# Another order for the first five tiles of a gated cross-attention and expert kernel

## The chip, the cores and the metric

The kernel runs on one core of a Trainium2 chip. Its time is the device time of one execution in microseconds (us); the median of three runs stands for the kernel. One further execution was recorded by the hardware profiler, and all times of single instructions come from it. The engines are PE (matmuls, with PEld for the loading of weights), DVE (vector), ACT (activations), POOL (general, and the issuer of indirect DMAs) and SP (issuer of plain DMAs).

## The reference

There are 4 sequences of 512 tokens, each token a vector of 256. Cut to what matters:

```python
def attend(q, kv_src, seg_id, Wq, Wkv, Wo):          # 16 heads of 16
    qh = split_heads(q @ Wq.T)
    k, v = split(kv_src @ Wkv.T, 2)
    gather = seg_id[:, :, None] - arange(4)          # four rows of kv_src for each token
    scores = einsum(qh, k[gather]) * 16 ** -0.5      # masked where gather < 0
    return einsum(softmax(scores), v[gather]) @ Wo.T

def experts(x, gate_w, w1, b1, w2, b2):              # 8 experts, 256 -> 1024 -> 256
    probs = softmax(x @ gate_w.T)
    weight = probs where among the two largest, else 0
    return sum_e weight[e] * (silu(x @ w1[e] + b1[e]) @ w2[e] + b2[e])

x = x + tanh(g_xattn) * attend(layernorm(x), ctx, itok, Wq, Wkv, Wo)
x = x + tanh(g_ffn) * experts(layernorm(x), ...)
```

All numbers are float32.

## The kernel before

The 2048 tokens are 16 tiles of 128. The kernel has two parts that overlap. The first goes over the tiles: attention, then the gate, then a scatter of every token's normalised row into a table `xs` in DRAM, once into the region of each of its two experts. The second goes over 37 blocks of 128 rows: it reads a block of `xs`, computes one expert on it, and adds the result to the output with an indirect DMA. A block can be read when the gate has been computed for enough tiles that it is surely full; the first three blocks are sure after tile 4 (`RAMP = 5`), and two more after each tile.

For a tile `t` the stages are these.

- `rows_of(t)`: an indirect DMA on POOL gathers the four rows of keys and values of each token into `g` (three buffers, 1 MB each; issued two tiles ahead). It reads a table `near` of the sequence, which `project_near` makes: a product on PE, a copy on ACT (`kv_near`), two stores by SP.
- `stage_ask(t)`: PE computes `pq`, the query and a part of the gate; ACT copies the gate's part to `asked`.
- `stage_attend(t)`: DVE computes `prod`, `sc` and the shifted scores; ACT the exponential `ex` (L459); DVE the sum `sm`, the weights `pr` and `v`. For the first four tiles the four parts of `v` are added on PE, later on DVE (`ao`). The generator yields twice before the sum, so that other work can be put in.
- `stage_out(t)`: PE transposes to `pa` (L497, L499), ACT copies to `aoT` (L512), PE computes `po` (L515), and DVE adds it to `x_sb` (L518), makes the gate's logits and the moments.
- `stage_route(g)`: for a group `g` of one or two tiles (tiles 0 and 1, tiles 2 and 3, then 4, 5, 6 and 7 alone): SP stores `x_sb`; DVE takes the two best experts (`best`, `which`, `pick`); PE counts ranks in `pp` (L568, L571); POOL computes the inverse root `rs` (`v_b` L266, `rs` L268) and writes the token numbers (L586); ACT the exponentials `exg` and the rows (L609); DVE the positions (`place`, `pos`), `nm` and the weights; and POOL issues two scatters for each tile (L377).
- `queue(tiles, w)`: DVE computes which expert and which row of `xs` the next `w` blocks take (`expert`, `row`). SP reads these, and fetches the block's weights `w1s` and its rows `xg`.

In a block PE transposes (`pxg` L783), DVE copies (`xgT` L786), PE computes the first product `ph` (L798), ACT the silu (L810), PE the second product `py` (L825).

The order on an engine is decided by a scheduler at build time, except that `in_order` chains the instructions traced within it: those of DVE only, when it is called without engines. `behind` puts one instruction behind another. The PSUM pool `ps_m` has two buffers, shared by `pa`, `po`, `pp` and the products of the near tables. SP also loads `xT`, `x` and the second weights `w2_sb`, where the loads of step `i` are tied to `prod` of tile `i` (`seen[i]`).

Of the kernel before, what the change touches and what calls it, by code (L numbers as in the profile page):

```python
# [23 lines left out]
def gated_xattn_moe(  # L24
# [29 lines left out]
    NT = NTOK // P  # L54
# [6 lines left out]
    RAMP = 5  # L61
    GROUPS = [(sum(sizes[:i]), n) for i, n in enumerate(sizes)]
    EDGE = KW - 1
    LKW = LKV + 2 * EDGE
    TOPK = 2
# [4 lines left out]
    PE, SP = mybir.EngineType.PE, mybir.EngineType.SP  # L70
# [3 lines left out]
    @contextmanager  # L74
    def in_order(*engines):

        traced = nc.cur_bb.bb.instructions
        old = {i.name for i in traced}
        yield
        for i in nc.cur_bb.bb.instructions:  # L80
            if i.name not in old and i.engine in (engines or (mybir.EngineType.DVE,)):
                if i.engine in order:
                    tc.add_manual_dep(i, order[i.engine].name, ORDER, reason="in this order")
                order[i.engine] = i
# [45 lines left out]
    src_rest = early_tile(KD * (B - 1) * P, "p (k b c) -> p k b c", k=KD, b=B - 1)  # L130

    def behind(i, *others, dep=ORDER):
        for other in others:
            tc.add_manual_dep(i, other.name, dep, reason="not in the way")
# [95 lines left out]
    def project_near(kv, psum, src, b, after=None):  # L230
        project(kv, psum, src, P, near[b], EDGE, f"near{b}", after)
        queue = nc.scalar if b == 0 else nc.sync
        return queue.dma_start(
            out=near[b][0:EDGE, :].unsqueeze(0),
            in_=kv[0:1, :].unsqueeze(1).to_broadcast([1, EDGE, 2 * D]),
        ).ins
# [48 lines left out]
    with tc.tile_pool(  # L285
# [26 lines left out]
        for m in range(KD):  # L312
            for k in range(KD):
                i = nc.tensor.matmul(
                    pwg[:, m, :],
                    wo_o[:, k, ts(m, P)],
                    wqg_sb[:, k, D:DG],
                    start=(k == 0),
                    stop=(k == KD - 1),
                ).ins  # L320
# [31 lines left out]
    def _layers(ctx, is_near):  # L352
# [10 lines left out]
        ps_m = pool("ps_m", 2, True)  # L363
# [7 lines left out]

        scatters, reads = [], []

        def scatter(rows, where):
            i = nc.gpsimd.indirect_dma_start(  # L377
                out=xs,
                out_offset=bass.IndirectOffsetOnAxis(ap=where, axis=0),
                in_=rows,  # L380
                in_offset=None,
            ).ins
            for other in scatters + reads:
                tc.declare_no_dep(i, other, reason="rows of their own")
            scatters.append(i)
# [24 lines left out]
        gathered, ops, asked, seen, exps, mvs, logits = {}, {}, {}, {}, {}, {}, {}  # L410
        group_of = {t: (g, t - t0) for g, (t0, n) in enumerate(GROUPS) for t in range(t0, t0 + n)}

        def rows_of(t):
            gt = gat.tile([P, KW, 2 * D], F32, tag="g", name=f"g_{t}")
            if is_near:
                i = gather_near(gt, t)
            else:
                i = gather(gt, every, B * LKW, idx_every[:, t : t + 1])
            gathered[t] = gt
            return i  # L420

        def stage_ask(t):

            pq = ps_q.tile([P, DG], F32, tag="q", name=f"pq_{t}")
            for k in range(KD):
                nc.tensor.matmul(  # L426
                    pq, xT_sb[:, t, k, :], wqg_sb[:, k, :], start=(k == 0), stop=(k == KD - 1)
                )
            asked[t] = small.tile([P, E], F32, tag="asked", name=f"asked_{t}")
            nc.scalar.copy(asked[t], pq[:, D:DG])  # L430
            ops[t] = pq
# [57 lines left out]
        def stage_out(t):  # L489
            ao = ops.pop(t)  # L490
            pa = ps_m.tile([P, KD, P], F32, tag="m", name=f"pa_{t}")
            parts = ao.shape[1]
            traced = len(nc.cur_bb.bb.instructions)
            for k in range(KD):
                for o in range(parts):
                    if parts == 1:
                        nc.tensor.transpose(pa[:, k, :], ao[:, o, ts(k, P)], ident)  # L497
                    else:
                        nc.tensor.matmul(  # L499
                            pa[:, k, :],  # L500
                            ao[:, o, ts(k, P)],
                            ident,
                            start=(o == 0),
                            stop=(o == parts - 1),
                        )
            if RAMP <= t and t + 1 in seen:

                for i in nc.cur_bb.bb.instructions[traced:]:
                    if i.engine == PE:
                        behind(i, seen[t + 1])  # L510
            aoT = att.tile([P, KD, P], F32, tag="aoT", name=f"aoT_{t}")
            nc.scalar.copy(aoT, pa)  # L512
            po = ps_m.tile([P, DG], F32, tag="m", name=f"po_{t}")
            for k in range(KD):
                nc.tensor.matmul(  # L515
                    po, aoT[:, k, :], wo_sb[:, k, :], start=(k == 0), stop=(k == KD - 1)
                )
            nc.vector.scalar_tensor_tensor(  # L518
                x_sb[:, t, :], po[:, 0:D], tg[:, 0:1], x_sb[:, t, :], ALU.mult, ALU.add
            )  # L520
            g, j = group_of[t]
            if j == 0:
                mvs[g] = stat.tile([P, GMAX, 2], F32, tag="mv", name=f"mv_{g}")
                logits[g] = gate.tile([P, GMAX, E], F32, tag="lg", name=f"lg_{g}")

            nc.vector.tensor_tensor(logits[g][:, j, :], po[:, D:DG], asked.pop(t), ALU.add)
            moments(mvs[g][:, j, :], x_sb[:, t, :], f"b{t}")


        def stage_route(g):  # L530

            t0, GT = GROUPS[g]
# [8 lines left out]
            row = gate.tile([P, GMAX, ROW], F32, tag="rows", name=f"rows_{g}", bufs=3)[:, 0:GT]  # L541
# [21 lines left out]
            for j in range(GT):  # L563
                t = t0 + j
# [14 lines left out]
            rs = stat.tile([P, GMAX], F32, tag="rs", name=f"rs_{g}")[:, 0:GT]  # L579
            nm = stat.tile([P, GMAX], F32, tag="nm", name=f"nm_{g}")[:, 0:GT]  # L580
            root = rsqrt(rs, mv, GT, f"b{g}")
            if t0 == RAMP - 1:

                for i in scatters[-TOPK * GROUPS[g - 1][1] // 2 :]:
                    behind(i, root)
            named = nc.gpsimd.tensor_copy(  # L586
                row_meta[:, :, :, 1].bitcast(I32),
                tokid[:, tiles].unsqueeze(2).to_broadcast([P, GT, E]),
            ).ins
            behind(named, root)  # L590
            for j in range(GT):
                nc.scalar.activation(ex[:, j, :], ex[:, j, :], AF.Exp, scale=rs[:, j : j + 1])
            yield
# [10 lines left out]
            pos = gate.tile([P, GMAX, TOPK], I32, tag="pos", name=f"pos_{g}")[:, 0:GT]  # L604
# [26 lines left out]
                tc.declare_no_dep(weighted, i, reason="other columns")  # L631
            for j in range(GT):
                for c in range(TOPK):
                    scatter(row[:, j, :], pos[:, j, c : c + 1])
            yield


# [247 lines left out]
        AHEAD = 2  # L885
# [10 lines left out]
        before = 0  # L896
        for i in range(NT + 1):
            if i + AHEAD < NT:
                gathers.append(rows_of(i + AHEAD))
            attend = stage_attend(i) if i < NT else iter(())  # L900
            queued = surely(i) if i in ends else 0
            with in_order():

                next(attend, None)
                if i != RAMP:
                    next(attend, None)
                if i < RAMP:
                    for _ in attend:
                        pass
                if i:  # L910
                    stage_out(i - 1)
                if i + 1 < NT:
                    stage_ask(i + 1)
                if i in ends:
                    for _ in stage_route(ends[i]):
                        pass
                if i >= RAMP and queued:
                    queue(i, queued - before)
                    before = queued
                if i == NT:  # L920
                    queue(i, NS - before, last=True)
                if i in (0, RAMP, RAMP + 2):
                    normalise_first(1 + (i + 1) // TPB)
                for _ in attend:
                    pass
            if is_near and i == 0:
                for b in range(1, B):
                    project_near(
                        kv_near[:, b, :], ps_m, src_rest[:, :, b - 1, :], b, after=exps[0]
                    )  # L930
            if i < E // 2:

                loads = [load_xT(i + 1), load_x(i + 2)] if i + 2 < B else []
                if i + 2 == B:
                    loads.append(load_xT(i + 1))
                for e in (2 * i, 2 * i + 1):
                    loads.append(nc.sync.dma_start(out=w2_sb[:, ts(e, NF), :], in_=w2[ts(e, P), :]).ins)
                for load in loads:
                    behind(load, seen[i], dep=SYNC)
# [91 lines left out]
```

## Time and profile before

| what | value |
|---|---|
| median of 3 runs | 398.99 us (397.7 to 399.93) |
| profiled execution: its own time | 399.22 us |
| profiled execution: span from first to last instruction | 397.5 us |
| mean granted clock of PE in it | 0.942 |
| busy: PE, DVE, ACT, POOL | 343.4, 195.7, 160.1, 131.3 us |
| first product of block 0 (`ph`) starts at | 85.24 us |

A line of the timeline reads: start in us, duration in us, engine, line of the code, operation, output and inputs with their shapes, count, and in brackets the idle time of the engine before it and what ended it. In the row of slices each digit is the busy share of a fortieth of the span (9.94 us) in tenths; `PEclk` is the granted clock of PE in tenths.

### The profile page before, as it was taken

Reading aid. Unit: us, or ns where it says so; the run is one execution under the profiler, and the core shown is the slowest. Engines: PE = TensorE matmul, PEld = TensorE weight load, DVE = VectorE, ACT = ScalarE, POOL = GpSimd, SP = SyncE. Lnnn points to the kernel's source line nnn. Section 1 sums busy time; section 2 is a strip of 40 time slices with the busy share of each in tenths; the row PEclk is TensorE's granted clock in tenths of the full one; section 3 lists DMA queues with packets and bytes.
Section 4 is the critical chain, followed back from the end, with each engine's and each line's share of the span. In section 5 each row is a group of like instructions: output and inputs, shape, how many; then the busy total and the mean of one; then the engine's idle time right before and its main releaser. Section 6 shows DMA issues by size and latency. Waiting matters only on the chain. (4 is left out here: it accounts for less than half of the span.)

```text
span 397.5 us, 7304 instructions
## 1 busy us (share of the span) xinstructions
PE 343.4 (86%) x2153; PEld 306.9 (77%) x2153; DVE 195.7 (49%) x663; ACT 160.1 (40%) x445; POOL 131.3 (33%) x164
## 2 busy tenths in 40 slices
PE   4877646089999989999999999999999999999960
PEld 1545534078998989898889989999999999999950
DVE  2288797879789989798947301101111111111000
ACT  1121202027756666767576334234243342342410
POOL 4421444513365354453724322112112122121311
PEclk9869696579999999999999999999999999999995
DMA  7899999589969988987667897776767767755111
GB/s 259 269 399 423 419 425 378 177 287 313 299 187 343 237 274 280 336 238 233 205 158 189 281 222 234 236 196 164 246 176 211 214 171 235 195 167 143 18 28 17
DMA packets 43577, 94.22 MB, mean 237 GB/s; under 512 B 14844, under 2 KB 31996, under 8 KB 35720
## 3 DMA queue, kind: packets, MB, share of 16 engines
q1 hardware_dynamic: 33506, 66.23, 51.2%
q0 software_dynamic: 9168, 26.09, 23.0%
q10 hardware_dynamic: 854, 1.33, 1.0%
q8 instruction: 21, 0.34, 0.3%
q14 instruction: 28, 0.23, 0.2%
HBM read 79.90 MB, written 13.73 MB: 236 GB/s over the span
## 5 line engine op out<-in xcount | busy, mean ns | idle before, releaser
L798 PE MATMUL ph<-xgT,w1s 128*128 128x128 f32 x1184 | 143.0, 276 | 0.0
L798 PEld LDWEIGHTS ph<-xgT,w1s 128*128 128x128 f32 x1184 | 140.3, 192 | 2.3
L825 PE MATMUL py<-w_sb,hT 128*128 x592 | 135.7, 380 | 1.4 <-DVE yw L836 0.7
L810 ACT ACTIVATE hT<-ph,b1s 128x128 f32<-128x128 f32 x296 | 83.6, 372 | 113.6 <-issue 95.7
L825 PEld LDWEIGHTS py<-w_sb,hT 128*128 128x128 f32 x592 | 109.2, 190 | 15.7 <-issue 2.1
L839 POOL DMA_INDIRECT out<-yw,ms x37 | 58.7, 1586 | 158.3 <-issue 69.5
L836 DVE SCALAR_TENSOR_TENSOR yw<-py,ms,b2s 128x256 f32<-128x256 f32 x37 | 17.8, 482 | 76.3 <-PE py L825 72.4
L786 DVE COPY xgT<-pxg 128x256 f32<-128x256 f32 x37 | 15.6, 421 | 69.5 <-PE pxg L783 69.4
L377 POOL DMA_INDIRECT xs<-rows,pos x32 | 35.0, 1094 | 30.6 <-ACT rows L609 7.3
L240 POOL DMA_INDIRECT g<-near,idx_near x16 | 17.6, 1098 | 37.4 <-DVE v L472 23.3
L439 DVE TENSOR_TENSOR prod<-pq,g 128x1024 f32<-128x1024 f32 x16 | 19.4, 1213 | 5.9 <-DMA g<-near,idx_near 5.9
L426 PE MATMUL pq<-wqg_sb,xT_sb 128*128 128x264 f32 x64 | 20.5, 449 | 1.5 <-DVE prod L439 1.1
L515 PE MATMUL po<-wo_sb,aoT 128*128 128x264 f32 x64 | 19.8, 436 | 2.0 <-ACT aoT L512 1.4
L472 DVE TENSOR_TENSOR v<-g,pr 128x1024 f32<-128x1024 f32 x16 | 19.6, 1224 | 0.5
L810 ACT ACT_TABLE_LOAD x13 | 16.7, 1283 | 7.7 <-issue 5.2
L442 DVE TENSOR_REDUCE sc<-prod 128x64 f32<-128x1024 f32 x16 | 19.5, 1217 | 0.4
L868 ACT ACTIVATE b2s<-b2s,ms 128x256 f32<-128x256 f32 x37 | 19.5, 532 | 0.0
L426 PEld LDWEIGHTS pq<-wqg_sb,xT_sb 128*128 128x128 f32 x64 | 14.0, 225 | 5.2 <-DVE prod L439 2.2
L497 PE MATMUL pa<-ident,ao 128*128 128x128 f32 x24 | 5.6, 308 | 13.2 <-DVE ao L485 13.1
L515 PEld LDWEIGHTS po<-wo_sb,aoT 128*128 128x128 f32 x64 | 12.1, 207 | 5.6 <-ACT aoT L512 4.0
L783 PE MATMUL pxg<-ident,xg 128*128 128x128 f32 x74 | 14.5, 278 | 1.5 <-DMA xg<-xs 1.5
L497 PEld LDWEIGHTS pa<-ident,ao 128*128 128x128 f32 x24 | 3.3, 165 | 14.5 <-issue 11.6
(128 smaller groups left out, 262.6 us busy)
## 6 DMA issues: line engine op xcount, KB each, us to landing
w1s<-in_w SPq DMA_DIRECT2D x37, 1024.0 KB, 5.4
w_sb<-in_w SPq DMA_DIRECT2D x8, 1024.0 KB
b2s<-in_b SPq DMA_DIRECT2D x37, 128.0 KB, 5.2
xg<-xs SPq DMA_DIRECT2D x37, 128.0 KB, 5.5
xT_sb<-in_xT SPq DMA_DIRECT2D x4, 512.0 KB, 11.3
x_sb<-in_x SPq DMA_DIRECT2D x4, 512.0 KB
out<-x_sb SPq DMA_DIRECT2D x6, 256.0 KB
xs<-padrow SPq DMA_DIRECT2D x9, 136.0 KB, 3.7
```

The costliest lines, as they stand in the source:

```text
L377: i = nc.gpsimd.indirect_dma_start(out=xs, out_offset=bass.IndirectOffsetOnAxis(ap=where, axis=0), in_=rows, in_offset=None,).ins
L426: nc.tensor.matmul(pq, xT_sb[:, t, k, :], wqg_sb[:, k, :], start=(k == 0), stop=(k == KD - 1))
L439: seen[t] = nc.vector.tensor_tensor(prod, pq[:, 0:D].unsqueeze(1).to_broadcast([P, KW, D]), gt[:, :, 0:D], ALU.mult).ins
L442: nc.vector.tensor_reduce(sc.rearrange("p o h -> p (o h)"), prod.rearrange("p o (h d) -> p (o h) d", d=HD), AX.X, ALU.add,)
L472: nc.vector.tensor_tensor(v.rearrange("p o (h d) -> p o h d", d=HD), gt[:, :, D : 2 * D].rearrange("p o (h d) -> p o h d", d=HD), pr.unsqu ...
L515: nc.tensor.matmul(po, aoT[:, k, :], wo_sb[:, k, :], start=(k == 0), stop=(k == KD - 1))
L798: m = nc.tensor.matmul(ph[:, i, :], w1s[:, k, ts(f, P)], xgT[:, k, :], start=(k == 0), stop=(k == KD - 1),).ins
L810: hidden = nc.scalar.activation(hT[:, f, :], ph[:, i, :], AF.Silu, bias=b1s[:, f : f + 1]).ins
L825: m = nc.tensor.matmul(py, hT[:, f, :], w2_sb[:, bass.ds(be_v * NF + f, 1), :].rearrange("p o d -> p (o d)"), start=(f == 0), stop=(f == N ...
L836: outs[s] = nc.vector.scalar_tensor_tensor(yw, py, ms[:, 0:1], b2s, ALU.mult, ALU.add).ins
L839: acc = nc.gpsimd.indirect_dma_start(out=out, out_offset=bass.IndirectOffsetOnAxis(ap=ms[:, 1:2].bitcast(I32), axis=0), in_=yw, in_offset= ...
L868: behind(nc.scalar.activation(b2s, b2s, AF.Copy, scale=ms[:, 0:1]).ins, hidden)
```

## The change

It touches the order of work in the first five tiles, and a little behind them.

- `stage_out` is cut into three: the transposes and the copy, `stage_project` (the product `po`) and `stage_add` (the sum, the logits and the moments).
- In tiles 0 to 4 the transposes of tile `i` come in step `i` itself, ahead of the ranks of the group that ends there, and its `po` behind these ranks. The sum of tile `i - 1` comes in step `i` behind the shifted scores, where ACT computes the exponential.
- In step 5 the products `prod` and `sc` of tile 5 are no longer taken first: the sum and the route of tile 4, the queue and the moments of the third sequence come ahead of them.
- The tables `near` of sequences 1 to 3 are made one each in steps 0, 1 and 2, instead of all three in step 0.
- PE's order is chained in steps 0 to 4, and POOL's in steps 0 to 5, gathers with it.
- The two scatters of tile 3 are held, and traced behind the `rs` and the token numbers of tile 4; before, `behind` put them behind that `rs`.

```diff
-        scatters, reads = [], []
+        scatters, reads, held = [], [], []
...
             nc.scalar.copy(aoT, pa)
+            ops[t] = aoT
+
+        def stage_project(t):
+            aoT = ops.pop(t)
             po = ps_m.tile([P, DG], F32, tag="m", name=f"po_{t}")
             for k in range(KD):
                 nc.tensor.matmul(
                     po, aoT[:, k, :], wo_sb[:, k, :], start=(k == 0), stop=(k == KD - 1)
                 )
+            ops[t] = po
+
+        def stage_add(t):
+            po = ops.pop(t)
             nc.vector.scalar_tensor_tensor(
...
-            if t0 == RAMP - 1:
-
-                for i in scatters[-TOPK * GROUPS[g - 1][1] // 2 :]:
-                    behind(i, root)
...
             behind(named, root)
+            while held:
+                scatter(*held.pop())
...
-                    scatter(row[:, j, :], pos[:, j, c : c + 1])
+                    if t0 + GT == RAMP - 1 and j:
+
+                        held.append((row[:, j, :], pos[:, j, c : c + 1]))
+                    else:
+                        scatter(row[:, j, :], pos[:, j, c : c + 1])
...
             if i + AHEAD < NT:
-                gathers.append(rows_of(i + AHEAD))
+                with in_order(*([mybir.EngineType.Pool] if i <= RAMP else [])):
+                    gathers.append(rows_of(i + AHEAD))
...
-            with in_order():
-
-                next(attend, None)
+            engines = [mybir.EngineType.DVE]
+            engines += [PE] if i < RAMP else []
+            engines += [mybir.EngineType.Pool] if i <= RAMP else []
+            with in_order(*engines):
+
                 if i != RAMP:
                     next(attend, None)
+                    next(attend, None)
+                if i > RAMP:
+                    stage_out(i - 1)
+                    stage_project(i - 1)
+                if i:
+                    stage_add(i - 1)
+                if i + 1 < NT:
+                    stage_ask(i + 1)
                 if i < RAMP:
                     for _ in attend:
                         pass
-                if i:
-                    stage_out(i - 1)
-                if i + 1 < NT:
-                    stage_ask(i + 1)
-                if i in ends:
-                    for _ in stage_route(ends[i]):
-                        pass
+                    stage_out(i)
+                route = stage_route(ends[i]) if i in ends else iter(())
+                next(route, None)
+                if i < RAMP:
+                    stage_project(i)
+                for _ in route:
+                    pass
+                if is_near and i + 1 < B:
+                    project_near(
+                        kv_near[:, i + 1, :], ps_m, src_rest[:, :, i, :], i + 1, after=exps[i]
+                    )
...
-            if is_near and i == 0:
-                for b in range(1, B):
-                    project_near(
-                        kv_near[:, b, :], ps_m, src_rest[:, :, b - 1, :], b, after=exps[0]
-                    )
```

## The prediction

> **What bounds the kernel now.** I read the page's slices first. PE is full from slice 8 (85 us) to the end and mostly idle before: the blocks of experts are a matmul stream, and what comes ahead of it only decides when it starts and with what beside it.
>
> ```profile
> PE   4877646089999989999999999999999999999960
> PEclk9869696579999999999999999999999999999995
> ```
>
> So I took the timeline of each engine from 20 us to the first block. PE shows how the stream starts: after 11 idle us come the transposes of block 0, then tile 5's output and tile 7's query, all at half clock (32 matmuls of `ph` take 3.73 us later, and four of `po` 1.16), then the first products at 85.24.
>
> ```profile
> 79.80 0.66 PE L497 MATMUL pa<-ident,ao 128*128 128x128 f32 x2 [10.67 <-DVE ao L485]
> 81.41 0.69 PE L783 MATMUL pxg<-ident,xg 128*128 128x128 f32 x2 [0.95 <-DMA xg<-xs]
> 81.89 1.97 PE L515 MATMUL po<-wo_sb,aoT 128*128 128x264 f32 x4
> 83.65 1.75 PE L426 MATMUL pq<-wqg_sb,xT_sb 128*128 128x264 f32 x4
> ```
>
> PE waited for xg, which SP could issue only at 79.32, when the last scatters had landed; the weights were asked for at 72.40.
>
> ```profile
> 72.40 0.37 SPq L752 DMA_DIRECT2D w1s<-in_w  x1
> 79.32 0.33 SPq L770 DMA_DIRECT2D xg<-xs  x1
> ```
>
> The scatters come from POOL, whose timeline shows no slack here: six scatters, one rsqrt and a copy in a row, with gaps of 0.2 to 0.3.
>
> ```profile
> 64.88 1.10 POOL L377 DMA_INDIRECT xs<-rows,pos  x1 [3.28 <-ACT rows L609]
> 66.29 0.97 POOL L377 DMA_INDIRECT xs<-rows,pos  x1 [0.30 <-issue]
> 67.53 0.19 POOL L266 TENSOR_SCALAR v_b<-mv 128x1 f32<-128x1 f32 x1 [0.27 <-DVE best L547]
> 67.80 0.62 POOL L268 TENSOR_TENSOR rs<-v_b,mhalf 128x1 f32<-128x1 f32 x1
> 68.61 1.06 POOL L377 DMA_INDIRECT xs<-rows,pos  x1 [0.20 <-issue]
> ...
> 72.71 0.96 POOL L377 DMA_INDIRECT xs<-rows,pos  x1 [0.30 <-issue]
> ```
>
> Ahead of that DVE is the bound, busy but for the exponential and the ranks (`sm`, `place`). Its lines for tile 4, and the copy and exponential of ACT beside them:
>
> ```profile
> 53.62 0.37 ACT L512 COPY aoT<-pa 128x256 f32<-128x256 f32 x1 [1.54 <-PE pa L499]
> 55.64 0.35 ACT L459 ACTIVATE ex<-sc,rsa 128x64 f32<-128x64 f32 x1 [1.65 <-DVE sc L455]
> 56.02 0.26 DVE L462 TENSOR_REDUCE sm<-ex 128x16 f32<-128x64 f32 x1 [0.41 <-ACT ex L459]
> 66.28 0.47 DVE L518 SCALAR_TENSOR_TENSOR x_sb<-po,tg,x_sb 128x256 f32<-128x256 f32 x1
> 69.44 0.15 DVE L607 SCALAR_TENSOR_TENSOR nm<-mv,rs 128x1 f32<-128x1 f32 x1
> ```
>
> **The change part by part.** No compute is added or taken away; all is order. I read the new order from the built program, engine by engine, and lay before's durations on it. The figure followed is the start of the six scatters, 64.88.
>
> *Outputs added while exponentials run, tiles 1 to 4.* The waits for the exponential (0.56, 0.41, 0.42, 0.41) go. But tile t-1's output is now added 3.27 us after its v ends (prod 1.22, sc 1.22, three small ones), and it is ready only after the transposes 2.02, copy 0.37, output 1.16 and four hand-overs, 3.9 at full clock. Tile 1: pa starts cold at 25.95 and output is there near 31.6, against 31.15: wait 0.5 for 0.56, 0. Tile 2: wait 0.6 for 0.41, +0.2. Tile 3: the route lies between, no wait, -0.4. Tile 4: ACT's new order has tile 4's exponential ahead of tile 3's aoT, which in before was copied at 53.62, two us earlier than it. So aoT starts 0.3 after `sc` is done, and output follows: 0.66 + 0.06 + 1.16 + 0.05 = 1.93 wait for 0.41: +1.5, and +2.5 if PE has gone cold (PE would be idle 3.4 us before it). I take +1.9.
>
> *Transposes ahead of ranks.* Ranks of tiles 0 and 1 now stand behind 2.02 us of pa, while picks take 1.7: wait 1.1 for 1.26, as PE is warm. Ranks of tiles 2 and 3 stand behind two transposes: 0.57 for 0.90. Together -0.5.
>
> *The near tables*, projected one per tile. On SP their stores stand behind the loads tied to tiles 0 and 1. Up to the first store 5.5 MB stand in SP's queue from 21.3 and 3.1 MB in POOL's; at the 0.42 MB/us of the saturated stretch (DMA share near 1.0 from 20 to 67) it lands near 42, where before it was there at 31. Tile 4's gather is held until then on POOL (issued at 34.38 before), and the rsqrt of tiles 0 and 1 behind it (41.80 before): rs near 45, when DVE's nm wants it: +0.4, between 0 and +2. The gather then has until 52 (9.2 us is its median): covered, with nothing to spare if it is issued after 43. The third near store waits for ACT at 48, with tile 12's xT and four w2 loads behind it (41.33 before): w2 is first read after 90, hidden; the DMA backlog that ended at 67.5 may end some 2 us later, under the first scatters.
>
> Start of the scatters: 0 + 0.2 - 0.4 + 1.9 - 0.5 + 0.4 = +1.6, 66.5.
>
> *Tile 4's output ahead of tile 5's products.* The 2.45 us of prod and sc leave DVE's way, and PE's output lies under the route: add at about 65.4 instead of 66.28. That gain meets POOL. Its new order from the first scatter on is scatter, scatter, the gather of tile 7 (issued at 58.36 before, 1.29 long), v_b, scatter, rs, copy, three scatters. The gather adds 1.5 with its gap, the third scatter 1.3 ahead of rs. So rs ends 3.54 + 2.8 = 6.35 after the start: 72.85. DVE's nm waits for it (69.44 before) and all of the queue (row, w1s' number) behind it: +3.4, w1s at 75.8, landing (5.4) by 81.2. Of the scatters the last ends 8.79 + 1.5 = 10.3 after the start, 76.8 for 73.67. From there to xg's issue 5.65 as before (w1s stands in the same place to them): 82.4. The early output is spent waiting.
>
> *The start of the stream.* xg lands 2.1 later, pxg 84.5, copied (0.42) by 85.65: first products at 85.7, for 85.24. But before had by then also done pa, po and pq; now they stand inside block 0, because tile 5 comes later: 0.4 + 1.05 + 1.05 = 2.5 at full clock. And in before they used up the cold clock; now block 0's products do. Clock rows: work from 42.91 was at full clock near 47.5, from 24.26 near 30.4, from 63.51 near 68, from 81.41 near 85.0: 3.6 to 6.2, mean 4.7, half lost: 2.35. The Trainium skill ("TensorE: Matmul & The Clock Gate", Part 1) says one busy window of about 3.4 us releases the clock, a loss of 1.7 at half rate; it also says that the window runs free of the program, so the wait may be longer. The trace's starts were longer, so I take 2.35; by 3.4 us the sum is 0.65 less.
>
> *After that* tile 5 is later by about what the stream is. DVE gets two copies of xgT put ahead of ranks and queue and waits for PE there; xg of block 3 (issued 99.07, used 104.60) has about its landing time of 5.5. I take +0.5 for stalls, 0 to +3. ACT gets 8 more table loads of 1.28 (59 for 51 over both branches of the program): covered by its idle time, half the stream. Regrouped later tiles: 0, within 1.
>
> Sum: 0.45 + 2.5 + 2.35 + 0.5 = +5.8. The profiled execution took 399.22 (span 397.5), 0.23 over the median; taken from 398.99 that is 404.8. A measurement of this kernel tells about 0.5%, 2.0 us, from no change.
>
> **Rivals.** *Faster: POOL's order doesn't bind.* If the spans of POOL's DMA instructions are mostly drawn and not spent, rs of tile 4 comes before 67.6, and the earlier output passes through. It decides there. Then DVE sets the chain; with the four exponential waits gone as meant (-1.8) and the 2.45 out of the way, products could start at 82.6 - 4.3 = 78.3; with pa, po, pq and the cold clock (4.9) that is 83.2 for 85.24: -2.0, 397.0. For it: POOL's spans are rough. Against it: before's third scatter started exactly where rs let it, and each next start is one span and 0.3 on.
>
> *No change.* The scatters start 0.9 early in the warm case of tile 4 and without the near wait, and land in 3.5 (median 4.7, least 2.4) instead of 5.65, if w1s comes behind them: 3.05 less than my sum, 0.65 less from the clock and no stalls (0.5): +1.6, 400.6. Against it: w1s and last scatter hang on the same rs.
>
> *Slower still: the near tables.* Gather 4 issued at 45 holds rs of tiles 0 and 1 until 47 (+2), and tile 4's products wait for its landing (+1), and blocks 3 and 5 stall: 405 + 3 = 408. For it: SP's queue is full to 67; against it: I count 42, not 45.
>
> **How the numbers follow.** Main case 0.62 (402 to 407), slower still 0.17, no change 0.14, faster 0.07. Predicted 404.8. The range takes in the main case and most of the slow one and the no-change one: 399.5 to 409.0; left out are the faster case and the ends, under 0.2. Slower by over 0.5% 0.79, within 0.14, faster 0.07.
>
> **What would show it.** POOL: six scatters from about 66.5 with a gather after the second, and rs of tile 4 ending near 73. DVE: a wait of 3 to 5 us at nm of tile 4 for POOL, and about 1.9 at tile 3's add for PE. PE: block 0's products about 85.7 at half clock, with pa, po and pq among them. ACT: aoT of tile 3 right behind an exponential. Wrong: nm without a wait, or the first products before 83; then the gather's place on POOL cost nothing. If the loss is there but nm is on time, it is in the near tables or the stream's stalls.

## Result and the profile after

The changed kernel takes 421.15 us (median of 4 runs, 420.47 to 421.38), the kernel before on the same chip 398.71. The ratio is 1.0559, with a 95% interval of 1.0526 to 1.0592: slower by 22.4 us, where +5.8 was predicted, and outside the stated range of 399.5 to 409.0. The profiled execution took 421.38 (span 419.7; before 399.22).

The slices of the page (10.5 us each, counted from 0) show that the stream of blocks still begins in slice 8, and that it now has gaps, in slice 10 (from 105 us) and slice 16 (from 168), with the clock low in slices 11 and 17, behind them.

```profile
PE   5448574289699989499999999999999999999970
PEclk9759965569969999979999999999999999999996
```

POOL's timeline has the order that was read from the built program: the gather after two scatters, `rs` of tile 4 behind a third.

```profile
67.41 1.10 POOL L377 DMA_INDIRECT xs<-rows,pos  x1 [5.53 <-ACT rows L615]
68.81 0.98 POOL L377 DMA_INDIRECT xs<-rows,pos  x1 [0.30 <-issue]
70.10 0.99 POOL L240 DMA_INDIRECT g<-near,idx_near  x1 [0.30 <-issue]
71.16 0.19 POOL L266 TENSOR_SCALAR v_b<-mv 128x1 f32<-128x1 f32 x1
71.62 1.01 POOL L377 DMA_INDIRECT xs<-rows,pos  x1 [0.27 <-issue]
72.65 0.60 POOL L268 TENSOR_TENSOR rs<-v_b,mhalf 128x1 f32<-128x1 f32 x1
...
76.38 0.96 POOL L377 DMA_INDIRECT xs<-rows,pos  x1 [0.30 <-issue]
```

DVE's timeline has the two waits that the prediction named, for PE at the add of tile 3 and for POOL at `nm` of tile 4. The second is shorter than the 3 to 5 us that were named, since DVE itself comes there later: the output of tile 4 is added at 67.22, not at 65.4.

```profile
58.72 0.48 DVE L526 SCALAR_TENSOR_TENSOR x_sb<-po,tg,x_sb 128x256 f32<-128x256 f32 x1 [2.92 <-PE po L519]
73.28 0.16 DVE L613 SCALAR_TENSOR_TENSOR nm<-mv,rs 128x1 f32<-128x1 f32 x1 [2.41 <-POOL rs L268]
```

PE's timeline shows the first products at half clock (ten take 2.50, and 1.28 before), with tile 5's output among them.

```profile
85.03 0.69 PE L793 MATMUL pxg<-ident,xg 128*128 128x128 f32 x2 [2.44 <-DMA xg<-xs]
86.24 2.50 PE L808 MATMUL ph<-xgT,w1s 128*128 128x128 f32 x10 [0.52 <-DVE xgT L796]
90.24 1.76 PE L519 MATMUL po<-wo_sb,aoT 128*128 128x264 f32 x4
```

So far it is the forecast. What it lacked is in PE's waits from 75 us on (columns: total, times, longest). Before, the same line read 1.5 us in two times.

```profile
PE pxg L793 <- DMA xg<-xs: 14.5, 5, 5.9
```

Blocks are counted from 0. In the kernel before PE had no wait at block 3:

```profile
104.60 0.38 PE L783 MATMUL pxg<-ident,xg 128*128 128x128 f32 x2
104.82 3.62 PE L825 MATMUL py<-w_sb,hT 128*128 x16
```

The two large waits of the changed kernel, at blocks 3 and 9, with what follows them on PE:

```profile
114.61 0.41 PE L793 MATMUL pxg<-ident,xg 128*128 128x128 f32 x2 [4.05 <-DMA xg<-xs]
114.86 2.94 PE L835 MATMUL py<-w_sb,hT 128*128 x8
...
119.72 5.00 PE L808 MATMUL ph<-xgT,w1s 128*128 128x128 f32 x32
...
179.37 0.66 PE L793 MATMUL pxg<-ident,xg 128*128 128x128 f32 x2 [5.93 <-DMA xg<-xs]
179.94 5.62 PE L835 MATMUL py<-w_sb,hT 128*128 x16
```

At full clock 8 `py` take 1.89, 16 take 3.62 and 32 `ph` 3.73. Block 3's wait costs 4.05 and about 3.3 of slow products, block 9's 5.93 and 2.0. Start of the transposes of a block (us), in the two kernels and in two of the experiments below:

| block | before | after | e1: tile 5 first again | e2: before, tile 5 last |
|---|---|---|---|---|
| 0 | 81.41 | 85.03 | 83.90 | 80.48 |
| 3 | 104.60 | 114.61 | 107.87 | 110.97 |
| 4 | 111.84 | 124.56 | 115.12 | 119.01 |
| 8 | 152.18 | 163.03 | 155.48 | 158.43 |
| 10 | 170.31 | 191.66 | 173.63 | 186.90 |

Why block 3's rows are late: ACT's timeline beside blocks 0 and 1. Between a silu and an exponential there stands a table load (`ACT_TABLE_LOAD`) each time.

```profile
89.99 1.28 ACT L820 ACT_TABLE_LOAD   x1
91.29 1.15 ACT L820 ACTIVATE hT<-ph,b1s 128x128 f32<-128x128 f32 x4
92.45 1.28 ACT L459 ACT_TABLE_LOAD   x1
93.75 0.35 ACT L459 ACTIVATE ex<-sc,rsa 128x64 f32<-128x64 f32 x1
94.10 1.28 ACT L820 ACT_TABLE_LOAD   x1
95.39 1.14 ACT L820 ACTIVATE hT<-ph,b1s 128x128 f32<-128x128 f32 x4
96.56 1.28 ACT L598 ACT_TABLE_LOAD   x1
97.85 0.30 ACT L598 ACTIVATE exg<-exg,rs 128x8 f32<-128x8 f32 x1
98.17 1.28 ACT L820 ACT_TABLE_LOAD   x1
...
102.18 0.63 ACT L615 ACTIVATE rows<-x_sb,nm,rs 128x256 f32<-128x256 f32 x1
```

In the kernel before, ACT did the exponential of tile 6, the gate's exponential and the rows of tile 5 ahead of the first silu:

```profile
84.53 0.35 ACT L459 ACTIVATE ex<-sc,rsa 128x64 f32<-128x64 f32 x1 [3.61 <-DVE sc L455]
...
86.57 0.30 ACT L592 ACTIVATE exg<-exg,rs 128x8 f32<-128x8 f32 x1 [0.97 <-POOL rs L268]
87.75 0.60 ACT L609 ACTIVATE rows<-x_sb,nm,rs 128x256 f32<-128x256 f32 x1 [0.88 <-DVE nm L607]
88.37 1.28 ACT L810 ACT_TABLE_LOAD   x1
89.67 2.18 ACT L810 ACTIVATE hT<-ph,b1s 128x128 f32<-128x128 f32 x8
```

POOL's timeline of the changed kernel has `rs` of tile 5 early, and then POOL stands idle for 9.28 us until those rows are there. (The bracket names DVE's `took`, which ended last, but in both kernels this scatter starts 0.79 after the rows end.)

```profile
93.58 0.59 POOL L268 TENSOR_TENSOR rs<-v_b,mhalf 128x1 f32<-128x1 f32 x1
...
103.60 1.05 POOL L377 DMA_INDIRECT xs<-rows,pos  x1 [9.28 <-DVE took L737]
```

Tile 5 by its steps:

| tile 5 | before | after | later by |
|---|---|---|---|
| `prod` starts (DVE) | 63.89 | 79.22 | 15.3 |
| output added (DVE) | 84.41 | 92.04 | 7.6 |
| gate's exponential (ACT) | 86.57 | 97.85 | 11.3 |
| rows (ACT) | 87.75 | 102.18 | 14.4 |
| first scatter (POOL) | 89.14 | 103.60 | 14.5 |
| `xg` of block 3 issued (SP) | 99.07 | 109.45 | 10.4 |

The 15.3 at the start had melted to 7.6 at the add; it is on ACT, between add and rows, that it doubled again. The 14.5 of the scatter are 10.4 at `xg`, because in the kernel before SP had `xg` behind the store of tile 6, for which it waited, and 8.6 after the start of tile 5's second scatter; in the changed kernel it follows that start by 4.5. Before:

```profile
98.13 0.35 SPq L537 DMA_DIRECT2D out<-x_sb  x1
99.07 0.33 SPq L770 DMA_DIRECT2D xg<-xs  x1
```

After:

```profile
109.45 0.33 SPq L780 DMA_DIRECT2D xg<-xs  x1
```

### The profile page after: what moved, and what is told of

Same layout as the page of the kernel before. It is cut to its first block, busy times and chain, and to the rows that moved or that the text cites. A ratio compares the mean times of both kernels' runs of the same rounds, so it can differ in the third digit from the quotient of the medians.

```text
span 419.7 us, 7304 instructions
## 1 busy us (share of the span) xinstructions
PE 349.0 (83%) x2153; PEld 311.5 (74%) x2153; DVE 196.1 (47%) x663; ACT 164.9 (39%) x449; POOL 130.3 (31%) x164
## 5 line engine op out<-in xcount | busy, mean ns | idle before, releaser
L808 PE MATMUL ph<-xgT,w1s 128*128 128x128 f32 x1184 | 145.0, 279 | 0.5 <-DVE xgT L796 0.5
L808 PEld LDWEIGHTS ph<-xgT,w1s 128*128 128x128 f32 x1184 | 142.9, 195 | 3.2 <-DVE xgT L796 0.9
L835 PE MATMUL py<-w_sb,hT 128*128 x592 | 140.4, 387 | 1.2 <-DVE yw L846 0.7
L820 ACT ACTIVATE hT<-ph,b1s 128x128 f32<-128x128 f32 x296 | 83.8, 372 | 101.6 <-issue 85.2
L835 PEld LDWEIGHTS py<-w_sb,hT 128*128 128x128 f32 x592 | 110.9, 194 | 16.0 <-issue 2.4
L793 PE MATMUL pxg<-ident,xg 128*128 128x128 f32 x74 | 14.9, 284 | 14.6 <-DMA xg<-xs 14.5
L512 ACT COPY aoT<-pa 128x256 f32<-128x256 f32 x16 | 6.0, 376 | 44.4 <-PE pa L497 33.5
L499 PE MATMUL pa<-ident,v 128*128 128x128 f32 x64 | 10.2, 326 | 15.8 <-DVE v L472 15.1
L499 PEld LDWEIGHTS pa<-ident,v 128*128 128x128 f32 x64 | 9.5, 234 | 17.7 <-DVE v L472 11.3
L793 PEld LDWEIGHTS pxg<-ident,xg 128*128 128x128 f32 x74 | 9.3, 146 | 16.5 <-issue 12.1
```

The costliest lines, as they stand in the source:

```text
L499: nc.tensor.matmul(pa[:, k, :], ao[:, o, ts(k, P)], ident, start=(o == 0), stop=(o == parts - 1),)
L793: nc.tensor.transpose(px[:, k, :], xg[:, ts(k, P)], ident)
L808: m = nc.tensor.matmul(ph[:, i, :], w1s[:, k, ts(f, P)], xgT[:, k, :], start=(k == 0), stop=(k == KD - 1),).ins
L820: hidden = nc.scalar.activation(hT[:, f, :], ph[:, i, :], AF.Silu, bias=b1s[:, f : f + 1]).ins
L835: m = nc.tensor.matmul(py, hT[:, f, :], w2_sb[:, bass.ds(be_v * NF + f, 1), :].rearrange("p o d -> p (o d)"), start=(f == 0), stop=(f == N ...
```

## The experiments

**e1 to e4: which part of the change costs the 22.4?** Theory A: tile 5's products behind the queue. Rivals: POOL's written order (B), the spread near tables (C).

e1, on the changed kernel, and e2, the other way round on the kernel before:

```diff
 e1, on the changed kernel
-                if i != RAMP:
-                    next(attend, None)
-                    next(attend, None)
+                next(attend, None)
+                if i != RAMP:
+                    next(attend, None)
 e2, on the kernel before
-                next(attend, None)
-                if i != RAMP:
-                    next(attend, None)
+                if i != RAMP:
+                    next(attend, None)
+                    next(attend, None)
```

> The changed kernel, with the products of tile 5 taken first in their step again (DVE's prod and weighted sum of tile 5 ahead of the adds of tile 4 and of the queue), all else as changed. Theory A (tile 5 behind the queue makes tiles 5 to 9 late, and PE then waits for the gathered rows of blocks 3 and 9, each time followed by half clock; worth some 16 us of the 22.4): 405, between 402 and 409, PE's waits for xg after the first products together under 3 us, add of tile 5 at 84 to 86 instead of 92. Theory B (POOL's written order, with the gathers and a held scatter in the chain, makes the later tiles late): no better than 417. Theory C (the near tables spread over the tiles disturb PE and ACT): no better than 417.

> The kernel before, with nothing changed but that the products of tile 5 come last in their step, behind tile 4's add, its route and the queue. Theory A: 413, between 409 and 417: the start of the first block's products stays at 85.2 within 0.5, and later blocks wait for their gathered rows, 10 us and more in sum. Theories B (POOL's order) and C (near tables): 399 to 402, since neither is in this kernel.

e1: 402.92 us against 398.62 (ratio 1.0117, 1.0068 to 1.0166). e2: 416.84 (1.0485, 1.0418 to 1.0552). The one edit is worth 22.4 - 4.3 = 18.1 us taken out of the changed kernel, and 18.2 put into the old one. Theory A holds; B and C, as the cause of the whole, fall. PE's waits for `xg` of e1 and of e2, from 75 us on:

```profile
PE pxg L793 <- DMA xg<-xs: 0.6, 2, 0.5
```

```profile
PE pxg L783 <- DMA xg<-xs: 15.2, 6, 6.1
```

e2's first block is even 0.9 earlier than before (table above), and its first products come at 81.68, not at the 85.2 expected, since PE's work for tile 5 no longer stands ahead of them. It loses all the same, at blocks 3 and 9: this loss has nothing to do with when the stream starts.

e3, POOL out of the chains, and e4, all near tables in the first step, both on the changed kernel:

```diff
 e3
-                with in_order(*([mybir.EngineType.Pool] if i <= RAMP else [])):
-                    gathers.append(rows_of(i + AHEAD))
+                gathers.append(rows_of(i + AHEAD))
...
-            engines += [mybir.EngineType.Pool] if i <= RAMP else []
 e4
-                if is_near and i + 1 < B:
-                    project_near(
-                        kv_near[:, i + 1, :], ps_m, src_rest[:, :, i, :], i + 1, after=exps[i]
-                    )
+            if is_near and i == 0:
+                for b in range(1, B):
+                    project_near(
+                        kv_near[:, b, :], ps_m, src_rest[:, :, b - 1, :], b, after=exps[0]
+                    )
```

> The changed kernel without POOL among the engines that keep the written order, in both places; tile 5 still last. Theory A: 418, between 415 and 421 (a gain of up to 3 us where the gathers go earlier, none of the waits for blocks 3 and 9 gone). Theory B: 403 to 407. Theory C: 420 to 421.

> The changed kernel with all near tables made in the first step as in the kernel before; tile 5 still last, POOL in the written order. Theory A: 420.5, between 418.5 and 422. Theory B: the same. Theory C: 403 to 410.

e3: 426.39 us (1.0728, 1.0656 to 1.0800). e4: 425.09 (1.0640, 1.0578 to 1.0701). Both are slower than the changed kernel, by some 5 and 4 us, outside what any theory gave (the intervals of e4 and of the changed kernel overlap a little, from 1.0578 to 1.0592, but every run of e4 is slower than every run of the changed kernel). So these two parts of the change do not cost the 22.4; with tile 5 last they help. In e3 the stream starts 3.0 earlier (82.02; 1.8 of it because the first gather landed earlier), but PE waits once more, at block 5:

```profile
134.22 0.66 PE L793 MATMUL pxg<-ident,xg 128*128 128x128 f32 x2 [4.46 <-DMA xg<-xs]
```

In e4 twelve near products in a row (5.31 us) stand ahead of tile 2's query, and DVE waits for it:

```profile
38.42 1.22 DVE L439 TENSOR_TENSOR prod<-pq,g 128x1024 f32<-128x1024 f32 x1 [3.13 <-ACT asked L430]
```

**e7, e9, e11: is it DVE's lateness, or ACT's order?** e7 puts, in e2, tile 5's rows ahead of block 1's silus (the gate's exponential, which its text names too, is not tied). e9 puts, in e2, three instructions of ACT ahead of block 0's silus, so that ACT's order at this place is that of the kernel before; e11 does the same in the changed kernel.

```diff
 e7 (late: the rows of tile 5), in the silus of up(s)
+                        if s == 1 and late:
+                            behind(hidden, *late)
 e9, e11 (late: the gate's exponential and the rows of tile 5)
+                        if s == 0 and late:
+                            behind(hidden, exps[RAMP + 1], *late)
```

> The kernel before with tile 5's products last, and in addition ACT takes tile 5's gate exponential and row copy ahead of the silus of block 1. Theory E (most of tile 5's lateness is not DVE's order itself, whose add is 2.8 us late, but that its rows then stand behind silus and table loads on ACT, 6 us from nm to rows): scatter of tile 5 about 5 us earlier, PE's wait of 4.4 at block 3 gone or under 1, 410, between 407 and 413. Rival (the lateness is DVE's and ACT's order matters little): 415 or more, with the wait at block 3 above 3.

> The kernel before with tile 5's products last, and ACT held to the order of the kernel before at this place: the exponential of tile 6 and the gate exponential and rows of tile 5 stand ahead of the first silus of block 0. Theory E, whole (a delay of 2.8 us at tile 5's add becomes 18 us only because ACT then takes silus and table loads first, for tile 5's rows and for tile 6's exponential): 404, between 401 and 408; scatter of tile 5 at 92 to 93.5 instead of 99.6, silus of block 0 some 4 us later, which PE pays once, and no wait above 2 us for the rows of blocks 3 and 9. Rival (the later blocks are late because DVE itself is behind, whatever ACT does): 410 or more, with a wait above 3 us at block 9.

> The changed kernel with the same three instructions of ACT ahead of the silus of block 0; tile 5's products still last. Theory E, whole: 408, between 404 and 413: the 4.3 us of the early part stay, block 0's silus come some 5 us later, and the waits of 4.05 and 5.9 at blocks 3 and 9 go. Rival: 417 or more.

e7: 411.16 us (1.0272, 1.0227 to 1.0317). The wait at block 3 is gone; those at blocks 7 and 9 stay (0.60, 4.35), since in that kernel the exponentials of tile 6 and of later tiles still stand behind silus: tile 6 is added at 108.66, against 97.62 before. e9: 406.73 (1.0189, 1.0145 to 1.0233). e11: 410.47 (1.0287, 1.0242 to 1.0331). So of the 18.2 us of e2, ACT's order is 10.3 (down to 7.9), and of the 22.4 of the changed kernel 10.8 (down to 11.6). Theory E holds for more than half, not whole: e9's rows come at 92.47, 4.7 later than before, and the silus wait for them. PE pays that once, as e9's list of waits says:

```profile
PE py L833 <- ACT hT L816: 2.8, 1, 2.8
```

The waits at blocks 3 and 9 are gone in e9 and in e11. PE's `xg` line, of e9 and then of e11, is left with waits at block 0 (2.25 and 2.42), at block 1 (1.25 and 1.07) and, in e9, 1.0 in a later one:

```profile
PE pxg L789 <- DMA xg<-xs: 4.5, 3, 2.2
```

```profile
PE pxg L799 <- DMA xg<-xs: 3.5, 2, 2.4
```

Nearly all of e9's 7.9 is lost before block 3: its transposes start at 111.64, 91.8 after tile 0's `prod`, where it was 84.6 in the kernel before. In this stretch lie the wait above, half clock behind it (0.50 from 94 to 100) and PE's work for tile 5, which the kernel before did ahead of its first products. How the 7.2 divide among these was not tested. Restoring ACT's order also takes the table loads from 30 back to 26; e7 keeps all 30 and is still some 6 us faster than e2, so that the place of tile 5's rows counts by itself.

**e8: do the transposes in front of ready products make it dear?** In the changed kernel the transposes of blocks 3 and 9 go behind the output products that stand after them.

```diff
 e8 (turns: the transposes of a block), at the end of down(s); m is its last py
+            for i in turns.get(s + 2, []) if s + 2 in (3, 9) else []:
+                behind(i, m)
```

> The changed kernel with the transposes of the gathered rows of blocks 3 and 9 behind the output products of the block before on PE's queue instead of among or ahead of them, so that PE has work while those rows are on their way. Theory F (the late rows cost as much as they do because the transposes stand in front of products that are ready: 10 and 16 of them, 2.4 and 3.6 us at full clock, and because PE then falls to half clock): 413, between 410.5 and 416; PE's waits for xg 14.5 to under 9, no py of block 8 above 0.3 us each. Rival (the rows are the bound whatever stands in PE's queue): 419 or more.

419.82 us (1.0457, 1.0411 to 1.0503): 413 was expected, and the theory falls in its size. The waits for `xg` shrank as it said, to 8.6 in all, but PE's timeline shows that the clock fell anyway, now under block 3's products (6.43 for 3.73):

```profile
114.12 0.69 PE L794 MATMUL pxg<-ident,xg 128*128 128x128 f32 x2 [1.17 <-DMA xg<-xs]
115.33 6.43 PE L810 MATMUL ph<-xgT,w1s 128*128 128x128 f32 x32 [0.51 <-DVE xgT L798]
```

Counted from tile 0's `prod`, block 10 began 5.4 us earlier than in the changed kernel (165.3 for 170.8), but block 15 only 0.3 (214.9 for 215.2): what was won was given back. The scheduler had moved later work too (e8 has 34 table loads for 30), and which of it took the gain back is open.

**e5, e6, e12, e13: the other 4.3 us.** e5 is e1 with POOL free. e6 has in addition tile 3's add behind tile 4's attention, and two of the scatters of tiles 2 and 3 behind `rs` of tile 4, both as before the change; e12 has only the first of these two edits, e13 only the second. All four have POOL free.

```diff
 e6, e12
-                if i:
+                if i and i != RAMP - 1:
                     stage_add(i - 1)
...
                     for _ in attend:
                         pass
+                    if i == RAMP - 1:
+                        stage_add(i - 1)
                     stage_out(i)
 e6, e13
+            if t0 == RAMP - 1:
+                for i in scatters[-TOPK * GROUPS[g - 1][1] // 2 :]:
+                    behind(i, root)
...
-            while held:
-                scatter(*held.pop())
...
-                    if t0 + GT == RAMP - 1 and j:
-                        held.append((row[:, j, :], pos[:, j, c : c + 1]))
-                    else:
-                        scatter(row[:, j, :], pos[:, j, c : c + 1])
+                    scatter(row[:, j, :], pos[:, j, c : c + 1])
```

> The changed kernel with the products of tile 5 first again and POOL out of the written order: what is left of the change is the early transposes, the adds during exponentials and the spread near tables. Theory D (of the 4.3 us that tile 5's return left, about half is POOL's order: the held scatter and the gather ahead of rs of tile 4, DVE's wait of 0.8 at nm there, and half is the 3.4 us that DVE waits at the add of tile 3): 400.7, between 399.5 and 402. Rival (POOL's order costs nothing once tile 5 is first): 402.5 to 403.5.

> As the one before it, but the add of tile 3 stands behind tile 4's attention again and half of the scatters stand behind rs of tile 4, as before the change. Theory D: DVE's wait of 3.4 at the add of tile 3 goes and one wait of 0.4 for an exponential comes back, 398, between 396.5 and 399.5, which is no loss and at most a small gain on the kernel before. Rival (PE's cold clock under the early transposes costs by itself): 400 to 402.

> Of the two edits that brought 402.3 back to 399.2, only one: the add of tile 3 stands behind tile 4's attention again; all four scatters of tiles 2 and 3 still stand ahead of rs of tile 4 on POOL. Theory G (nearly all of the 3.1 us is the wait of 3.4 at the add of tile 3): 399.7, between 398.8 and 400.5. Rival (the scatters ahead of rs hold DVE at nm of tile 4 and share the loss): 401 to 402, with a wait of over 1 us at that nm.

> The other one of the two edits: two of the four scatters of tiles 2 and 3 stand behind rs of tile 4 on POOL again, and the add of tile 3 stands ahead of tile 4's attention, as changed. Theory H (what is left of the loss, 0.6% of the time, is the scatters' place, and DVE's wait at the add of tile 3 costs nothing that can be measured): 399.5 to 400.3, DVE's wait at nm of tile 4 gone. Rival (both edits are needed, since the wait at the add of tile 3 moves into one at nm of tile 4 and back): 401.5 to 402.5.

| | add of tile 3 | scatters | us | ratio to before |
|---|---|---|---|---|
| e5 | early | all ahead of `rs` | 402.34 | 1.0064 (1.0043 to 1.0085) |
| e12 | as before | all ahead of `rs` | 402.30 | 1.0055 (1.0031 to 1.0080) |
| e13 | early | two behind `rs` | 399.94 | 1.0039 (1.0020 to 1.0057) |
| e6 | as before | two behind `rs` | 399.22 | 1.0006 (0.9984 to 1.0029) |

The times are medians, the ratios are of means. Only e6 cannot be told from the kernel before; e5 and e12 lie above its interval, e13 overlaps both. So theory D's end is right (what remains of the change with both edits costs nothing and brings nothing that can be measured), but not its 400.7 for e5. Theory G falls: the add alone changes nothing that the times can tell, though DVE's wait of 3.38 there is gone and the one at `nm` of tile 4 has not grown (0.83 for 0.73). H holds in its median but not in its ratio. In the profiled executions both edits do move the stream: block 10 starts at 173.66 in e5, 171.82 in e12, 171.88 in e13 and 169.70 in e6, with tile 0's `prod` at 20.2 in all four. How the 2.5 us by which e5 is slower divide between the two stays open. Whether POOL's chain costs anything once tile 5 is first (e1 against e5) stays open too: the intervals overlap. No version was found that beats the kernel before.

## Why the prediction was wrong, step by step

*Right.* The direction, though on its own grounds for the smaller part only (16.4 of the 22.4 us come from elsewhere), and the sum up to block 3. Without its wait block 3's transposes would have begun at 110.56, 6.0 after those of before, 0.9 of which is a later first gather (`prod` of tile 0 at 20.91 for 20.01). The 5.1 that is left stands against 0.45 + 2.5 + 2.35 = 5.3. The match is good to about 1 us, not better: by then PE had also done six `py` more than the kernel before (1.3 us) and not yet tile 6's ranks (0.6), and the cold clock lasted 6.6 us from block 0's transposes on, where 4.7 had been taken. The single terms: last scatter ends 77.34 (forecast 76.8), w1s 76.40 (75.8), xg 82.78 (82.4), first products 86.24 (85.7).

*The step that failed* is "After that", which gave +0.5, 0 to +3, for all that tile 5's later place does to the stream once it runs. It measured 16.4 us: 22.4 less the 6.0 by which block 3 was late without its wait. (The 18 of e1 and e2 also hold what tile 5's place does ahead of block 3: 1.4 in e1, counted from tile 0's `prod`.) One clause of it was right and not followed, two were wrong.

"xg of block 3 ... has about its landing time": read rightly. Landings of `xg` in the kernel before took 5.0 us at the least and 5.5 in the median, so that the 5.5 between issue and use held half a us of slack at most, and an `xg` that is later than the stream had to show as a wait. It was issued 10.4 later into a stream 6.0 later, and PE waited 4.05.

"Later by about what the stream is": wrong. It was taken from the whole, and not followed through tile 5's own steps. They are 7.6 late at the add and 14.5 at the scatter.

"8 more table loads ... covered by its idle time": wrong. The share of idle time was read, not the place. The new loads were the sign that exponentials had moved in between silus. The Trainium skill ("ScalarE: Activation LUTs", What ACT_TABLE_LOAD costs) gives 2.66 us for each switch with a drain; the rows here show 1.28 and the next instruction 0.01 to 0.02 later, so the measurement decides. The executed branch has 30 loads for 26: four more cost ACT 5.1 us by the row, and 10.6 by the page's figure (an estimate). Over the whole stream, in which ACT is idle more than half, that would be covered. But five loads, 6.4 us, stand in the 12.2 us from 89.99 to tile 5's rows at 102.18, with silus between them, where the kernel before had none ahead of the rows. It is their place that makes them dear: e9 and e11 take 10 to 11 us back by ACT's order.

*Mis-sized inside the right part.* Tile 3's add: a wait of 2.92 was measured, at the upper end of the 1.9 to 2.9 that the two cases give. ACT did take the exponential ahead of `aoT`, as said (55.89 and 56.15), but this is not needed for the wait: in e5 `aoT` comes first, and the wait is 3.38, because PE had been idle for 3.5 us and transposes at half clock (16 matmuls in 3.75). And taking it away alone (e12) gains nothing that the times can tell. Near tables: +0.4 was put on them as a cost; by e4, spreading them saves about 4 in this order.

*The rivals.* POOL's order does bind, as argued against the faster case: `nm` of tile 4 waits for POOL's `rs`, and without the chain (e3) the stream starts 1.2 earlier, the first gather set aside. The slower one named stalls of blocks 3 and 5, but gave them to the near tables and put no price of their own on them: its 3 us are the two waits of 2 and 1.

## What to carry to other kernels

When a change puts a producer later, follow that producer through every engine's new order to the transfer that its consumer waits for, and compare with when the consumer now arrives; an interval equal to the landing time is no slack. A count of table loads that rises in the built program is a sign that two kinds of work have been interleaved on one engine: look at which result now stands behind which, not at the engine's idle share. A wait on one engine that is easily seen (3.4 us here) can be worth less than the times can tell, and one edit of a large reordering can carry four fifths of its cost, so test the edits one by one in both directions.

## What had not been expected of the hardware

A gap's length alone does not say whether or when PE falls to half clock. In the changed kernel a wait of 1.44 at block 7 (152.68) left the granted clock at 1.00 in every 3 us around it; in e8 a wait of 1.17 ahead of block 3's transposes was followed by more than 6 us at 0.50, the transposes included (0.69). Nor does the fall come at the end of the gap. After the wait of 4.05 at block 3 the transposes still ran at full speed (0.41) and the clock fell about 1 us after the gap had ended; after the wait of 5.93 at block 9 the transposes were slow already (0.66). What decides it was not tested.
